# An LSTM step's attention sums, gate transpose and filler products rearranged in a four-layer kernel

## The chip, the cores and the metric

The kernel runs on one core of a Trainium2 chip, as one program. The metric is the device time of one execution in microseconds; lower is better. A core has TensorE (PE, matrix products, with weight loads shown apart as PEld), VectorE (DVE), ScalarE (ACT), GpSimd (POOL) and queues of DMA transfers, most of them issued by SyncE (SP). Each engine works through its own instructions in order and waits on semaphores for the others.

## What is computed

The reference is a chain of four layers on x (4 sequences of 512 tokens, 256 wide) with a context of 64 tokens per sequence. Each layer adds a gated attention-like part and a gated feed-forward part. Only the first layer matters here. Its attention part is a two-layer LSTM with attention over the context, and its feed-forward part is a mixture of 8 experts, of which the two best are summed per token:

```
for t in 512 steps:                                   # h, c: 4 x 256
    e     = tanh(ctx @ Wf + (h @ Wh)[:, None] + b)    # 4 x 64 x 256
    alpha = softmax(e @ v)                            # 4 x 64
    gates = [x_t, alpha @ ctx] @ W_ih0.T + h @ W_hh0.T + b
    i, f, g, o = split(gates)
    c = sigmoid(f) * c + sigmoid(i) * tanh(g)
    h = sigmoid(o) * tanh(c)
    (the second LSTM cell uses h and c of this step, not of an earlier one)
x = x + tanh(g_xattn[0]) * h2
x = x + tanh(g_ffn[0]) * mixture(layernorm(x))        # 8 experts, 256 -> 1024 -> 256, gelu
```

Everything is in fp32 in this part.

## The kernel before

The steps of the LSTM depend on each other, so `recurrence` calls `lstm_step` 512 times. The second cell and the mixture of experts of a block of 64 steps need nothing of later steps. They are cut into small tasks (`block_tasks`), which a planner, `Later`, puts into the holes of the following steps. `lstm_step` calls `later.fill(engine, budget)` at fixed places: each call hands out tasks of that engine, in the order of their kinds, until the budget is spent. For TensorE a mixture product (L720 up, L751 down: a 128x128 weight times 256 columns) costs 1; the three places are called slots A, B and C with budgets of 1, 2 and 2. An fp32 product is recorded as two passes. What is left behind the last step is put out by `later.drain()`, with nothing else beside it; then the next layers begin. All instructions of a step are pinned in program order, so each engine's queue has the order of the code.

One step, with the lines of the profile:

- L816 multiplies h by Wh (`psa`); VectorE transposes the result to `hw` (L821), which holds one number per partition, unit chunk c, and sequence.
- L825 adds h times W_hh to the gates in PSUM (`psf`). Then slot A.
- L833: two sums of VectorE, one for each pair p of sequences, add hw to the projected context `fproj`; the tile `e` is 128 partitions x [pair p, chunk c, sequence b in the pair, 64 context tokens]. L834 is the tanh of pair 0 (256 columns), L836 two tanh for pair 1, one per chunk (128 columns).
- L843: small products of `e` with v give the scores `psr` of each pair, pair 0 first, both chunks into one sum. Then slot B.
- L854 takes the maximum of a pair's scores, L855 the exp with its sum (the maximum enters as a bias operand). ScalarE may do one task of the planner here, among them the mixture's gelu (L730).
- L861 to L863 transpose and normalise to `alb`; L867 adds the attended context's share to `psf`. VectorE's task and slot C follow.
- L875 transposes `psf` to `gt`, all four gates at once. L474 starts the next step's gates with x's share. L878 is one tanh over the four gates (a sigmoid is a tanh of half its argument), L882 and L886 the new cell state, L888 its tanh `tcn`, L893 the new hidden state `hb`.
- If a task has changed ScalarE's table of functions (gelu), L891 runs a dummy exp on one element (`spare`) after `tcn`, so that the table of exp and tanh is loaded there and not in the path of the next step.

GpSimd copies the cell state (L894); SP's tasks, four a step, load the experts' weights and store blocks.

Of the kernel before, what the change touches and what calls it, by code (L numbers as in the profile page):

```python
# [24 lines left out]
AF = mybir.ActivationFunctionType  # L25
# [5 lines left out]
NB, S, D = 4, 512, 256  # L31
SC = 64
# [5 lines left out]
KD = D // P  # L38
NE = 8

SLOT_A, SLOT_B, SLOT_C = 1, 2, 2
ROUND = 1.5 * 2.0**23
F_MOE = (1024, 512, 1024)

# [96 lines left out]
def bc(ap, axis, n):  # L141

    ap = ap.unsqueeze(axis)
    shape = list(ap.shape)
    shape[axis] = n
    return ap.to_broadcast(shape)
# [214 lines left out]
def recurrence(net, w, pools):  # L361
# [22 lines left out]
    for t in range(S):  # L384
        i, u = divmod(t, P)
        if u == 0 and i + 1 < TPB:
            norm_x(net, later, w, pools, xb, i + 1)
        v = t % TB
        if v == 0:
            n = t // TB  # L390

            assert n < 3 or all(x["at"] for x in used[n - 3])
            hb = two.tile([P, 2, TB, NB], FP, name="hb", bufs=3)
            cb = two.tile([P, 2, TB, NB], FP, name="cb", bufs=3)
        if t % 32 == 0 and t and t // 32 + 1 < NJ:
            gates_of_block(net, later, w, pools, xb, ge, t // 32 + 1)
        lstm_step(net, pools["step"], ps, w, later, ge, t, h, hb[:, :, v], cb[:, :, v], ga[t % 2], ga[1 - t % 2])
        h = hb[:, :, v]
        if t > TB and t % 8 == 4:
            net.fill()  # L400
        if v == TB - 1:
            used.append(block_tasks(net, later, w, moe0, pools, n, hb, cb))
# [67 lines left out]
def gates_of_x(net, out, ge, t):  # L470

    sel = net.ident.rearrange("p (b t) -> p b t", b=NB)[:, :, t % 32]
    for q in range(4):
        net.tc.keep_in_program_order(net.nc.tensor.matmul(  # L474
            out[32 * q : 32 * q + NB, :], lhsT=sel, rhs=ge[t // 32][:, ts(q, 256)],
            start=True, stop=False,
        ))
# [330 lines left out]
def lstm_step(net, sp, ps, w, later, ge, t, h, hnew, cnew, ga, ganext):  # L808
    nc = net.nc
    pin = net.tc.keep_in_program_order  # L810
    psf = ps["f"]
    later.step += 1

    for c in range(2):
        for q in range(4):
            pin(nc.tensor.matmul(  # L816
                ps["a"][32 * q : 32 * q + NB, :], lhsT=h[:, c, :], rhs=w["wh"][:, c, ts(q, 64)],
                start=c == 0, stop=c == 1,
            ))
    hw = sp.tile([P, 2, 32], FP, name="hw")  # L820
    pin(nc.vector.transpose(hw.rearrange("p c b -> p (c b)"), ps["a"]))  # L821

    for c in range(2):
        for q in range(4):
            pin(nc.tensor.matmul(  # L825
                psf[32 * q : 32 * q + NB, :], lhsT=h[:, c, :], rhs=w["whh"][:, c, ts(q, 256)],
                start=False, stop=False,
            ))
    later.fill("PE", SLOT_A)

    e = sp.tile([P, 2, 2, 2, SC], FP, name="e")
    for p in range(2):
        pin(nc.vector.tensor_add(e[:, p], w["fproj"][:, p], bc(hw[:, :, ts(p, 2)], 3, SC)))  # L833
    pin(nc.scalar.activation(e[:, 0], e[:, 0], AF.Tanh))  # L834
    for c in range(2):
        pin(nc.scalar.activation(e[:, 1, c], e[:, 1, c], AF.Tanh))  # L836

    for p in range(2):
        for c in range(2):
            for b in range(2):  # L840
                ev = e[:, p, c, b].rearrange("p (i s) -> p i s", i=2)
                for i in range(2):
                    pin(nc.tensor.matmul(  # L843
                        ps["r"][p][ts(2 * b + i, 32), :], lhsT=w["vrep"][:, c, :],
                        rhs=ev[:, ::-1, :] if i else ev, start=c == 0, stop=c == 1,
                    ))
    later.fill("PE", SLOT_B)

    stat = sp.tile([P, 2, 3], FP, name="stat")
    al = sp.tile([P, 2, SC], FP, name="al")  # L850
    alT = sp.tile([P, 2, 32], FP, name="alT")
    alb = sp.tile([P, 2, NB], FP, name="alb")
    for p in range(2):
        pin(nc.vector.tensor_reduce(stat[:, p, 0:1], ps["r"][p], AX.X, ALU.max, negate=True))  # L854
        pin(nc.scalar.activation(  # L855
            al[:, p], ps["r"][p], AF.Exp, bias=stat[:, p, 0:1], accum_out=stat[:, p, 1:2]
        ))
    later.table = None
    later.fill("ACT", 1)
    for p in range(2):  # L860
        pin(nc.vector.transpose(alT[:, p], al[:, p, 0:32]))  # L861
        pin(nc.vector.reciprocal(stat[:, p, 2:3], stat[:, p, 1:2]))
        pin(nc.vector.scalar_tensor_tensor(  # L863
            alb[:, p], alT[:, p, 0:NB], stat[:, p, 2:3], w["own"][:, p], ALU.mult, ALU.mult
        ))
        for q in range(4):
            pin(nc.tensor.matmul(  # L867
                psf[32 * q : 32 * q + NB, :], lhsT=alb[:, p], rhs=w["fw"][:, p, ts(q, 256)],
                start=False, stop=p == 1,
            ))  # L870
    later.fill("DVE", 1)
    later.fill("PE", SLOT_C)

    gt = sp.tile([P, 8, 32], FP, name="gt")
    pin(nc.vector.transpose(gt.rearrange("p g b -> p (g b)"), psf))  # L875
    if t + 1 < S:
        gates_of_x(net, psf, ge, t + 1)
    pin(nc.scalar.activation(  # L878
        ga[:, 0:4].rearrange("p g c b -> p (g c) b"), gt[:, :, 0:NB], AF.Tanh, scale=0.5
    ))  # L880
    u = sp.tile([P, 2, 2, NB], FP, name="u")
    pin(nc.vector.scalar_tensor_tensor(  # L882
        u.rearrange("p g c b -> p g (c b)"), ga[:, 0:2].rearrange("p g c b -> p g (c b)"), 1.0,
        ga.rearrange("p (s x) c b -> p s x (c b)", x=2)[:, 1:3, 0], ALU.add, ALU.mult,
    ))
    pin(nc.vector.scalar_tensor_tensor(ganext[:, 4], u[:, 1], 0.5, u[:, 0], ALU.mult, ALU.add))  # L886
    tcn = sp.tile([P, 2, NB], FP, name="tcn")
    pin(nc.scalar.activation(tcn, ganext[:, 4], AF.Tanh, scale=0.5))  # L888
    if later.table:

        pin(nc.scalar.activation(w["spare"][0:1, 0:1], w["spare"][0:1, 1:2], AF.Exp))  # L891
        later.table = None
    pin(nc.vector.scalar_tensor_tensor(hnew, ga[:, 3], 1.0, tcn, ALU.add, ALU.mult))  # L893
    pin(nc.gpsimd.tensor_copy(cnew, ganext[:, 4]))  # L894
    later.fill("POOL", 1)
    later.fill("SP", 4)
# [1286 lines left out]
```

## Time and profile before

| what | value |
|---|---|
| median of 14 runs | 5411.22 us (5404.61 to 5414.55) |
| the profiled execution | 5411.6 us, its span 5409.9 us |
| busy share of the span | PE 85%, PEld 46%, DVE 45%, ACT 47%, POOL 9% |
| mean granted TensorE clock | 0.964 of full |
| first and last hidden state of the LSTM written at | 55.8 us and 3461.0 us |
| last product of the mixture behind the last step ends at | 3622 us |
| step length, plain median | 6.5 to 6.6 us |

The page gives, for the slowest core, the busy time of each engine, the same in 40 slices, the chain of work that ended last, and the costliest groups of instructions by line. A group's line has the number of instructions, their busy time, the mean ns of one, then the engine's idle time just before them and what ended most of it. The trace behind the page can be asked for the instructions in a stretch of time (the timeline) and for busy time by stretch (the windows). "Busy" for PE means that a product is in flight, not that the array is at its peak. A matrix product on four column groups at a time is noted 128*4 or 128*32.

### The profile page before, as it was taken

How to read it: one execution, taken by the hardware profiler on the slowest of the kernel's cores; microseconds unless marked ns; L12 is line 12 of the kernel's file. 1: busy time of each engine (PE TensorE's matmuls, PEld its weight loads, DVE VectorE, ACT ScalarE, POOL GpSimd, SP SyncE). 2: the span in 40 equal slices, each digit the busy share in tenths (PEclk: the TensorE clock that was granted, in tenths of full speed). 3: DMA queues.
4: the chain of work that ended last, by engine and by line, in shares of the span. 5: the costliest groups of instructions: out<-in, count | busy, mean ns of one | idle time of the engine just before them, and what ended most of it. 6: DMA issues, size and time to landing. Idle time of an engine off the chain costs nothing. (4 is left out here: it accounts for less than half of the span.)

```text
span 5409.9 us, 139195 instructions
## 1 busy us (share of the span) xinstructions
PE 4587.2 (85%) x57504; PEld 2502.5 (46%) x57504; DVE 2441.7 (45%) x9780; ACT 2532.8 (47%) x7118; POOL 465.9 (9%) x884
## 2 busy tenths in 40 slices
PE   5556699789999899999999989996989599979967
PEld 2222244334444344444444434673543366768744
DVE  3555555555555555555555555314433333221145
ACT  2233366555566556656556556511247366223212
POOL 1000100100000100000000000101011201130030
PEclk8999999999999999999999999997999799989978
DMA  5000012121122122122122111222454334553210
GB/s 194 2 2 2 2 72 94 64 75 72 73 97 111 42 88 95 72 82 80 65 89 95 72 63 44 89 89 74 168 175 149 132 118 142 201 175 137 95 53 8
DMA packets 117964, 480.46 MB, mean 89 GB/s; under 512 B 23473, under 2 KB 62787, under 8 KB 87939
## 3 DMA queue, kind: packets, MB, share of 16 engines
q1 hardware_dynamic: 105026, 437.85, 22.6%
q0 software_dynamic: 12288, 33.57, 1.8%
q8 instruction: 455, 7.45, 0.6%
q14 instruction: 195, 1.59, 0.1%
HBM read 434.65 MB, written 137.89 MB: 106 GB/s over the span
## 5 line engine op out<-in xcount | busy, mean ns | idle before, releaser
L867 PE MATMUL psf<-fw,alb 128*4 128x256 f32 x8192 | 537.7, 379 | 172.6 <-DVE alb L863 142.0
L720 PE MATMUL ps_up<-xm,ring 128*128 128x256 f32 x2048 | 614.8, 412 | 3.4 <-ACT h L730 3.3
L751 PE MATMUL ps_down<-ring,h 128*128 128x256 f32 x2048 | 582.2, 400 | 0.0
L825 PE MATMUL psf<-whh,hb 128*4 128x256 f32 x8176 | 537.4, 380 | 0.0
L720 PEld LDWEIGHTS ps_up<-xm,ring 128*128 128x128 f32 x2048 | 335.9, 188 | 226.7 <-issue 174.2
L855 ACT ACTIVATE al<-psr,stat 128x64 f32<-128x64 f32 x1024 | 313.3, 310 | 270.0 <-DVE stat L854 269.4
L834 ACT ACTIVATE e<-e 128x256 f32<-128x256 f32 x512 | 213.4, 417 | 465.2 <-DVE e L833 464.2
L751 PEld LDWEIGHTS ps_down<-ring,h 128*128 128x128 f32 x2048 | 357.8, 190 | 156.9 <-issue 111.5
L854 DVE TENSOR_REDUCE stat<-psr 128x1 f32<-128x64 f32 x1024 | 229.4, 225 | 416.8 <-PE psr L843 406.2
L833 DVE TENSOR_TENSOR e<-fproj,hw 128x256 f32<-128x256 f32 x1024 | 395.4, 427 | 17.6
L816 PE MATMUL psa<-wh,hb 128*4 128x64 f32 x8176 | 208.4, 219 | 230.0 <-DVE hb L893 229.4
L843 PE MATMUL psr<-e,vrep 128*32 128x64 f32 x16384 | 349.1, 224 | 49.1 <-ACT e L834 43.6
L894 POOL COPY cb<-ga 128x8 f32<-128x8 f32 x512 | 97.0, 189 | 3230.6 <-DVE ga L886 3230.6
L474 PE MATMUL psf<-ge,ident 128*4 128x256 f32 x4096 | 317.9, 382 | 65.4 <-DVE gt L875 65.2
L843 PEld LDWEIGHTS psr<-e,vrep 128*32 128x32 f32 x16384 | 261.4, 109 | 238.2 <-ACT e L834 230.4
L878 ACT ACTIVATE ga<-gt 128x32 f32<-128x32 f32 x512 | 116.8, 228 | 540.6 <-DVE gt L875 540.4
L875 DVE STREAM_TRANSPOSE gt<-psf 128x256 f32<-128x256 f32 x512 | 230.4, 450 | 302.0 <-PE psf L867 301.6
L1717 ACT ACTIVATE h<-featT,txtT 128x512 f32<-128x512 f32 x512 | 323.6, 710 | 72.9 <-PE psr L936 60.0
L867 PEld LDWEIGHTS psf<-fw,alb 128*4 128x4 f32 x8192 | 116.8, 84 | 518.2 <-DVE alb L863 516.8
L936 PE MATMUL ps_up<-xT,ring 128*128 128x256 f32 x1280 | 310.7, 395 | 42.4 <-DVE xT L1354 30.3
L816 PEld LDWEIGHTS psa<-wh,hb 128*4 128x4 f32 x8176 | 113.7, 85 | 487.3 <-DVE hb L893 487.3
L936 PEld LDWEIGHTS ps_up<-xT,ring 128*128 128x128 f32 x1280 | 246.2, 197 | 119.8 <-DVE xT L1354 31.9
(418 smaller groups left out, 6552.6 us busy)
## 6 DMA issues: line engine op xcount, KB each, us to landing
ring<-in_L_w_dram SPq DMA_DIRECT2D x208, 1024.0 KB, 4.8
ring<-in_L_w_dram SPq DMA_DIRECT2D x120, 512.0 KB, 4.0
res<-y SPq DMA_DIRECT2D x120, 128.0 KB, 1.7
rows_in<-rows SPq DMA_DIRECT2D x40, 256.0 KB, 3.8
rows_in<-rows SPq DMA_DIRECT2D x40, 128.0 KB, 2.9
rows<-in_x_dram SPq DMA_DIRECT2D x2, 1920.0 KB, 31.7
res<-in_x_dram SPq DMA_DIRECT2D x2, 1920.0 KB, 15.5
xtok<-in_x_dram SPq DMA_DIRECT2D x4, 512.0 KB, 6.0
```

The source lines that it names most:

```text
L474: net.tc.keep_in_program_order(net.nc.tensor.matmul(out[32 * q : 32 * q + NB, :], lhsT=sel, rhs=ge[t // 32][:, ts(q, 256)], start=True, st ...
L720: yield nc.tensor.matmul(cell["ps"][:, f % 2, :], lhsT=ex["w"][:, k, ts(f, P)], rhs=box["x"][:, k, :], start=k == 0, stop=k == KD - 1,)
L751: yield nc.tensor.matmul(cell["ps"], lhsT=ex["h"][:, f, ts(p, P)], rhs=ex["down"][:, f, :], start=f == 0, stop=f == 7,)
L816: pin(nc.tensor.matmul(ps["a"][32 * q : 32 * q + NB, :], lhsT=h[:, c, :], rhs=w["wh"][:, c, ts(q, 64)], start=c == 0, stop=c == 1,))
L825: pin(nc.tensor.matmul(psf[32 * q : 32 * q + NB, :], lhsT=h[:, c, :], rhs=w["whh"][:, c, ts(q, 256)], start=False, stop=False,))
L833: pin(nc.vector.tensor_add(e[:, p], w["fproj"][:, p], bc(hw[:, :, ts(p, 2)], 3, SC)))
L843: pin(nc.tensor.matmul(ps["r"][p][ts(2 * b + i, 32), :], lhsT=w["vrep"][:, c, :], rhs=ev[:, ::-1, :] if i else ev, start=c == 0, stop=c == ...
L855: pin(nc.scalar.activation(al[:, p], ps["r"][p], AF.Exp, bias=stat[:, p, 0:1], accum_out=stat[:, p, 1:2]))
L867: pin(nc.tensor.matmul(psf[32 * q : 32 * q + NB, :], lhsT=alb[:, p], rhs=w["fw"][:, p, ts(q, 256)], start=False, stop=p == 1,))
L875: pin(nc.vector.transpose(gt.rearrange("p g b -> p (g b)"), psf))
L936: return lambda *a, **k: self.tc.keep_in_program_order(fn(*a, **k))
L1717: nc.scalar.activation(h, featT[:, ec, :], AF.Tanh, bias=w["txtT"][:, ec, col : col + 1])
```

## The change

Four things change in `lstm_step`. First, a quarter of the attention's sums (pair 0, chunk 0) is not added by VectorE: two tanh of 64 columns, one per sequence, read `fproj` and take the column of hw as their bias operand. Second, the other three quarters are three sums of 128 columns, each followed by its own tanh, instead of two sums of 256 and tanh of 256, 128 and 128. Third, the transpose of the gates and their tanh are split into i, f, g (192 columns) and o (64 columns), and both tanh are queued before the next step's L474. Fourth, slot A is gone, so a step takes up to four mixture products instead of five; the number of products stays. In the changed kernel the bias tanh are L832, the three sums L836 and their tanh L837; further down line numbers shift by 1 to 4: the scores are L844, the maximum L855, exp L856, `alb` L864, L867 becomes L868, the transposes are L877, the gates' tanh L880, `u` L886, `tcn` L892, the dummy L895, the hidden state L897.

```diff
-SLOT_A, SLOT_B, SLOT_C = 1, 2, 2
+SLOT_B, SLOT_C = 2, 2
...
-    later.fill("PE", SLOT_A)
 
     e = sp.tile([P, 2, 2, 2, SC], FP, name="e")
-    for p in range(2):
-        pin(nc.vector.tensor_add(e[:, p], w["fproj"][:, p], bc(hw[:, :, ts(p, 2)], 3, SC)))
-    pin(nc.scalar.activation(e[:, 0], e[:, 0], AF.Tanh))
-    for c in range(2):
-        pin(nc.scalar.activation(e[:, 1, c], e[:, 1, c], AF.Tanh))
+    for b in range(2):
+        pin(nc.scalar.activation(
+            e[:, 0, 0, b], w["fproj"][:, 0, 0, b], AF.Tanh, bias=hw[:, 0, b : b + 1]
+        ))
+    for p, c in ((0, 1), (1, 0), (1, 1)):
+        pin(nc.vector.tensor_add(e[:, p, c], w["fproj"][:, p, c], bc(hw[:, c, ts(p, 2)], 2, SC)))
+        pin(nc.scalar.activation(e[:, p, c], e[:, p, c], AF.Tanh))
...
-    pin(nc.vector.transpose(gt.rearrange("p g b -> p (g b)"), psf))
+    for lo, hi in ((0, 6), (6, 8)):
+        pin(nc.vector.transpose(
+            gt[:, lo:hi].rearrange("p g b -> p (g b)"), psf[:, 32 * lo : 32 * hi]
+        ))
+        pin(nc.scalar.activation(
+            ga.rearrange("p g c b -> p (g c) b")[:, lo:hi], gt[:, lo:hi, 0:NB], AF.Tanh, scale=0.5
+        ))
     if t + 1 < S:
         gates_of_x(net, psf, ge, t + 1)
-    pin(nc.scalar.activation(
-        ga[:, 0:4].rearrange("p g c b -> p (g c) b"), gt[:, :, 0:NB], AF.Tanh, scale=0.5
-    ))
```

## The prediction

> **What bounds the kernel now.** I read the page's busy shares first (PE 85%, everything else below half), then its chain of waits. That chain covers only the last 200 us, in the layers behind the LSTM, which the change does not touch, so it says nothing here. The waits by engine then led to the LSTM lines: each step's engines wait for one another in turn. The timeline of one ordinary step, from one hidden state to the next, shows it (start us, duration us, engine, line, operation, tile; xN merges N instructions; in brackets the idle time before and who ended it):
>
> ```profile
> 1627.44 0.25 DVE L821 STREAM_TRANSPOSE hw<-psa 128x64 f32<-128x64 f32 x1 [0.53 <-PE psa L816]
> 1627.72 0.76 DVE L833 TENSOR_TENSOR e<-fproj,hw 128x256 f32<-128x256 f32 x2
> 1628.16 0.70 PE L720 MATMUL ps_up<-xm,ring 128*128 128x256 f32 x2
> 1628.24 0.42 ACT L834 ACTIVATE e<-e 128x256 f32<-128x256 f32 x1 [1.53 <-DVE e L833]
> 1628.57 0.49 ACT L836 ACTIVATE e<-e 128x128 f32<-128x128 f32 x2
> 1628.79 0.49 PEld L843 LDWEIGHTS psr<-e,vrep 128*32 128x32 f32 x32 [0.33 <-ACT e L834]
> 1629.29 0.45 DVE L854 TENSOR_REDUCE stat<-psr 128x1 f32<-128x64 f32 x2 [0.81 <-PE psr L843]
> 1630.76 0.22 DVE L863 SCALAR_TENSOR_TENSOR alb<-alT,stat,own 128x4 f32<-128x4 f32 x1
> 1631.73 0.45 DVE L875 STREAM_TRANSPOSE gt<-psf 128x256 f32<-128x256 f32 x1 [0.74 <-PE psf L867]
> 1632.28 0.23 ACT L878 ACTIVATE ga<-gt 128x32 f32<-128x32 f32 x1 [1.96 <-DVE gt L875]
> 1633.33 0.17 DVE L893 SCALAR_TENSOR_TENSOR hb<-ga,tcn 128x8 f32<-128x8 f32 x1 [0.34 <-ACT tcn L888]
> ```
>
> The reader is to see a serial chain in which the mixture's products (L720, L751) fill PE's holes. It is a chain of latencies: steps without any product take 6.50 us, steps with five 6.59. The one in slot A (at 1628.16) holds up the scores: L843 starts 0.13 after L834 ended, against 0.05 in steps without it.
>
> After the last step the products left over run with nothing beside them (windows; columns are length, then busy time and count of PE, PEld, DVE, ACT, POOL, then the granted clock):
>
> ```profile
> 3461.00:3541.00 80.00, 78.06 (x364) 66.42 (x363) 11.58 (x45) 28.13 (x59) 11.21 (x10) 1.00 0.39 135
> 3541.00:3622.00 81.00, 78.44 (x360) 67.72 (x358) 7.71 (x18) 17.83 (x42) 0.00 (x0) 1.00 0.23 80
> ```
>
> PE is busy for 156.5 of 161 us: here a product is paid in full.
>
> **Kinds of step.** Where a step has a gelu (L730), ScalarE loads its table before it and loads the old one back (L891) after `tcn`, into the next step:
>
> ```profile
> 2051.04 1.28 ACT L891 ACT_TABLE_LOAD   x1
> 2051.05 0.17 DVE L893 SCALAR_TENSOR_TENSOR hb<-ga,tcn 128x8 f32<-128x8 f32 x1 [0.28 <-ACT tcn L888]
> 2051.75 0.25 DVE L821 STREAM_TRANSPOSE hw<-psa 128x64 f32<-128x64 f32 x1 [0.53 <-PE psa L816]
> 2052.33 0.20 ACT L891 ACTIVATE spare<-spare 1x1 f32<-1x1 f32 x1
> ```
>
> After a gelu step ScalarE is free only 1.11 us after the hidden state, although hw is there at 0.78. Before, that was hidden, since the first tanh waited for VectorE's sum until 1.27. Four kinds by this, with their median length in the trace: plain 219 (105 at 6.50 without products, 114 at 6.59), gelu after plain 77 (6.66), gelu after gelu 139 (6.54), plain after gelu 77 (41 at 6.40, 36 at 6.26). Sum 3343 us; the trace has 60 us more in starts of blocks and table changes, which I leave as they are. In the changed program's order of instructions the counts are 259, 76, 101 and 76.
>
> **Part 1, the attention's sums.** Removed: two sums of 256 columns and three tanh. Added: two tanh of 64 columns with hw as bias, which need no sum, three sums and three tanh of 128. The price is that of a tanh with a bias operand from SBUF. The step has none, but a later layer has (groups by line, the second number behind the bar is the mean ns; then a timeline of four in a row):
>
> ```profile
> L1717 ACT ACTIVATE h<-featT,txtT 128x512 f32<-128x512 f32 x512 | 323.6, 710 | 72.9 <-PE psr L936 60.0 <-DVE featT L1705 12.8
> L836 ACT ACTIVATE e<-e 128x128 f32<-128x128 f32 x1024 | 254.6, 295 | 1.9 <-DVE e L833 1.9
> L855 ACT ACTIVATE al<-psr,stat 128x64 f32<-128x64 f32 x1024 | 313.3, 310 | 270.0 <-DVE stat L854 269.4
> ```
> ```profile
> 4008.68 2.56 ACT L1717 ACTIVATE h<-featT,txtT 128x512 f32<-128x512 f32 x4 [2.02 <-DVE featT L1705]
> ```
>
> Plain tanh: from `tcn` (8 columns, 209 ns) to L834 (256 columns, 417 ns) it is 0.84 ns a column; L836's two starts lie 0.20 apart. With a bias: median 707 ns for 512 columns, starts 0.61 apart (four in 2.56 with the last one's 0.71), so 0.10 of each is overlapped. 448 columns fewer at 0.84 leave 0.33, and the next start after 0.24. If the bias operand cost nothing it would be L836's 0.20 less 64 columns: 0.15. L855, also with a bias and 64 columns, but out of PSUM, takes 0.31, so 0.21. Not overlapped at all it would be 0.33. I take 0.24, as L1717 is the same operation out of the same memory; 0.15 and 0.33 are the ends.
>
> The Trainium skill ("ScalarE: Activation LUTs", What ACT_TABLE_LOAD costs) speaks against the change at this point: each pointer operand adds about 93 ns, and an activation with a pointer bias takes 280 ns and 0.833 a column, 333 ns here. By that estimate rather than L855's row the sum below is 25 us higher; it leaves my figure where it is.
>
> *Plain step*, in us after the hidden state. hw is complete at 0.78; ScalarE answers VectorE after 0.03, and after 0.06 more where it waits for two semaphores, as L834 did and the first bias tanh does. So the tanh start at 0.87, 1.11, 1.35 (ends 1.65), 1.55 and 1.75 (ends 2.05). VectorE's sums are never last: one of 256 takes 0.43, starts 0.34 apart; at the 1.04 ns a column between the transposes of hw (64 columns, 250 ns) and `gt` (256, 450) one of 128 takes 0.29, 0.21 apart, done by 1.10, 1.31 and 1.52. From the end of the last tanh of a half to its maximum L854 there are 0.44 (2.15 to 2.59 in steps without products). So the first L854 starts at 2.09, against 2.38 with a product in slot A and 2.30 without; the second at 2.49, which still meets the second exp's slot with 0.1 to spare. From the first L854 to `gt` it is 2.44, a chain on ACT and DVE. Behind L843's added waits on PE stand the other scores, slot B's products and L867, which needs `alb` (1.33 after the first L854: 3.42) and those products: last score pass 2.20, then 0.15, 0.32, 0.22, 0.22 and 0.31, the spacings of the trace: 3.42 too. So they just don't bind. `gt` starts at 4.53 instead of 4.82 or 4.74.
> *After a gelu*: the first bias tanh starts at 1.22 (1.11 and 0.11 for the small activation), 0.35 later than in a plain step. First L854 at 2.43, against 2.38 or 2.24; L867 by the same sum at 3.75 instead of 3.65, and from it 2.76 to the next hidden state, less part 2: 6.43.
> *Gelu steps*: here `ga` waits for table load and two gelus, which follow the second exp; they shift with it: from 3.40 to 3.14 after plain, from 3.34 to 3.48 after gelu.
>
> **Part 2, the gates.** `gt` takes 450 ns for 256 columns and hw 250 for 64, so 192 take 0.38: the tanh of i, f, g starts 0.07 earlier, wherever ScalarE is free, not in gelu steps. The second transpose and the tanh of o end about 0.9 after `gt` started; `tcn` wants ScalarE at 1.3: hidden, while nothing delays `tcn`. L474 waits for the second transpose, but PE is on slot C's products until later anyhow.
>
> **Part 3, four products.** Slot A's delay is in the lengths above. But the work stays: by the programs' orders 340 products lay behind the last step, and now 643 do. 303 products are 606 passes; successive passes in the drain start 0.216 apart: 131 us, and 160 us of drain have about 5 us of waits for ScalarE's gelus, so 136. Nothing can hide it: PE works in order and the next layer is behind it. The Trainium skill ("TensorE: Matmul & The Clock Gate", Back-to-back issue gap) would have N/2.4 + 2.5 = 109 ns for 256 columns, 66 us for the lot and a change that gains; the row, in fp32, is twice that and decides.
>
> **Sum.** New lengths: plain 6.59 - 0.29 - 0.07, rounded to 6.22 (6.50 - 0.21 - 0.07 is 6.22); gelu after plain 6.66 - 0.26 = 6.40; gelu after gelu 6.54 + 0.14 = 6.68; plain after gelu 6.43. 259 x 6.22 + 76 x 6.40 + 101 x 6.68 + 76 x 6.43 = 3261, 82 to 83 us less than 3343. The profiled execution took 5411.6 (span 5409.9), 0.4 above the median: 5411.6 - 83 + 136 - 0.4 = **5464 us**.
>
> **Rivals.**
> *Faster: the bias operand costs nothing.* At 0.15 per bias tanh each step is 0.19 shorter, 96 us in all: 5368. For it: the operand could be fetched while the engine waits. Against: L1717's starts are 0.61 apart in a full queue. It decides from 0.19 per bias tanh downward: there the step's gain pays for the drain.
> *Gain and drain cancel*, within 0.2%, which is about what a measurement of this kernel tells from no change: 0.18 to 0.20 per bias tanh: 5400 to 5422. L855's 0.21 with a drain at the bare 131 is still 5434.
> *Dearer: a bias tanh doesn't overlap* (0.33): 0.19 more in each step, 5561; ScalarE free only when the small activation has ended (1.31) adds 0.09 to 177 steps: 5480.
> *The change doesn't get its parts early*, if L843 waited for all of e: the order shows a wait at each part, so I give it nothing of its own.
>
> **Chances.** Forecast (5422 to 5505) 0.72; dearer 0.08; cancel 0.08; faster 0.12. The range 5400 to 5505 leaves out 0.2 at its two ends. Faster by over 0.2%: 0.12; within: 0.08; slower: 0.80.
>
> **What would show it.** Bias tanh 0.33 long, the next 0.24 after it; plain steps near 6.2 us; steps after a gelu no shorter; L843's first wait ended by the bias tanh or the (0,1) part; the last hidden state at about 3378 us instead of 3461, and then a drain of about 296 us at full clock instead of 161. Wrong if the tanh are spaced 0.15, if the gelu-after-gelu steps shorten, or if the granted clock falls in the longer drain.

## The result and the profile after

The changed kernel takes 5471.5 us (median of 6 runs, 5464.9 to 5477.2), against 5411.5 before (median of 28): ratio 1.0111, 95% interval 1.0101 to 1.0121. It is slower by 60 us; the forecast was 5464, slower by 53. The profiled execution took 5467.2, 55.6 more than that of before, so the traces account for 55.6 of the 60, and the profile is among the shorter runs.

Where it went, from the two traces (us):

| stretch | before | after | difference | forecast |
|---|---|---|---|---|
| up to the first hidden state | 55.8 | 54.3 | -1.5 | 0 |
| 511 further steps | 3405.2 | 3319.6 | -85.6 | -83 |
| products behind the last step, to VectorE's last sum of them (L758) | 160.6 | 303.2 | +142.6 | +136 |
| the next layers to the end of the span | 1788.3 | 1788.4 | +0.1 | 0 |

An ordinary step after the change, in the timeline (some of its lines are left out; start us, duration us, then as in the step shown of before; the hidden state before it was complete at 1615.58):

```profile
1616.10 0.25 DVE L821 STREAM_TRANSPOSE hw<-psa 128x64 f32<-128x64 f32 x1 [0.53 <-PE psa L816]
1616.39 0.70 DVE L836 TENSOR_TENSOR e<-fproj,hw 128x128 f32<-128x128 f32 x3
1616.45 0.59 ACT L832 ACTIVATE e<-fproj,hw 128x64 f32<-128x64 f32 x2 [1.07 <-DVE hw L821]
1616.85 0.99 PEld L844 LDWEIGHTS psr<-e,vrep 128*32 128x32 f32 x32 [0.46 <-ACT e L832]
1616.94 0.69 ACT L837 ACTIVATE e<-e 128x128 f32<-128x128 f32 x3
1617.67 0.23 DVE L855 TENSOR_REDUCE stat<-psr 128x1 f32<-128x64 f32 x1 [0.59 <-PE psr L844]
1619.15 0.22 DVE L864 SCALAR_TENSOR_TENSOR alb<-alT,stat,own 128x4 f32<-128x4 f32 x1
1620.11 0.52 DVE L877 STREAM_TRANSPOSE gt<-psf 128x192 f32<-128x192 f32 x2 [0.35 <-PE psf L868]
1620.59 0.34 ACT L880 ACTIVATE ga<-gt 128x24 f32<-128x24 f32 x2 [1.86 <-DVE gt L877]
1621.63 0.17 DVE L897 SCALAR_TENSOR_TENSOR hb<-ga,tcn 128x8 f32<-128x8 f32 x1 [0.34 <-ACT tcn L892]
```

The reader is to see three things. ScalarE now works from 0.87 us after the hidden state (1616.45) instead of 1.33, released by hw itself. The two bias tanh together take 0.59 us although they hold only 64 columns each, and the next tanh can start only 0.49 after the first of them. The first maximum starts at 2.09 instead of 2.38, and the hidden state is complete 6.22 us after the last one instead of 6.59.

The same engine in a step that follows a gelu (timeline of ScalarE; the hidden state was complete at 1596.23):

```profile
1596.05 1.28 ACT L895 ACT_TABLE_LOAD   x1
1597.35 0.20 ACT L895 ACTIVATE spare<-spare 1x1 f32<-1x1 f32 x1
1597.45 0.57 ACT L832 ACTIVATE e<-fproj,hw 128x64 f32<-128x64 f32 x2
1597.93 0.69 ACT L837 ACTIVATE e<-e 128x128 f32<-128x128 f32 x3
```

Here L832 has no bracket: it didn't wait for hw, it waited for its own engine. VectorE's sum could have been done in that time for nothing, so the bias should buy no start and cost its price; the experiment with four plain quarters below shows it.

Behind the last step (windows; columns as in those of before):

```profile
3384.00:3530.00 146.00, 140.85 (x648) 120.39 (x648) 16.61 (x55) 39.77 (x90) 11.20 (x10) 1.00 0.39 134
3530.00:3677.00 147.00, 143.20 (x657) 123.72 (x655) 11.67 (x26) 34.06 (x82) 0.00 (x0) 1.00 0.34 117
```

PE is busy for 284 of 293 us at full clock, nearly twice the time of before. Median lengths by kind of step, with what was forecast:

| kind | before | after | forecast |
|---|---|---|---|
| plain, with products / without | 6.59 / 6.50 | 6.23 / 6.23 | 6.22 |
| gelu after plain | 6.66 | 6.41 | 6.40 |
| gelu after gelu | 6.54 | 6.69 | 6.68 |
| plain after gelu, with products / without | 6.40 / 6.45 | 6.44 / 6.38 | 6.43 |

("With products" means at least two of them. The 6.45 is the middle of only 16 steps, which lie between 6.26 and 6.59.)

### The profile page after: what moved, and what is told of

The parts are those of the page before. It is cut to its first block, busy times and chain, and to the rows that moved or that the text cites. A ratio compares the mean times of both kernels' runs of the same rounds, so it can differ in the third digit from the quotient of the medians.

```text
span 5465.5 us, 142169 instructions
## 1 busy us (share of the span) xinstructions
PE 4736.5 (87%) x57504; PEld 2657.6 (49%) x57504; DVE 2443.7 (45%) x10804; ACT 2683.6 (49%) x8540; POOL 467.1 (9%) x884
## 3 DMA queue, kind: packets, MB, share of 16 engines
q1 hardware_dynamic: 105026, 437.85, 22.5%
## 5 line engine op out<-in xcount | busy, mean ns | idle before, releaser
L844 PE MATMUL psr<-e,vrep 128*32 128x64 f32 x16384 | 592.5, 231 | 49.5 <-ACT e L832 46.8
L868 PE MATMUL psf<-fw,alb 128*4 128x256 f32 x8192 | 537.8, 379 | 100.5 <-DVE alb L864 95.9
L844 PEld LDWEIGHTS psr<-e,vrep 128*32 128x32 f32 x16384 | 390.2, 108 | 409.8 <-ACT e L832 286.8
L720 PE MATMUL ps_up<-xm,ring 128*128 128x256 f32 x2048 | 546.9, 398 | 8.7 <-ACT h L730 8.3
L751 PE MATMUL ps_down<-ring,h 128*128 128x256 f32 x2048 | 542.5, 396 | 0.0
L832 ACT ACTIVATE e<-fproj,hw 128x64 f32<-128x64 f32 x1024 | 297.9, 337 | 362.8 <-DVE hw L821 362.7
L880 ACT ACTIVATE ga<-gt 128x24 f32<-128x24 f32 (+1 forms) x1024 | 170.7, 214 | 569.5 <-DVE gt L877 568.3
L855 DVE TENSOR_REDUCE stat<-psr 128x1 f32<-128x64 f32 x1024 | 230.2, 225 | 446.8 <-PE psr L844 446.8
L720 PEld LDWEIGHTS ps_up<-xm,ring 128*128 128x128 f32 x2048 | 356.7, 189 | 143.2 <-issue 79.8
L856 ACT ACTIVATE al<-psr,stat 128x64 f32<-128x64 f32 x1024 | 321.5, 314 | 180.7 <-DVE stat L855 180.7
L877 DVE STREAM_TRANSPOSE gt<-psf 128x192 f32<-128x192 f32 (+1 forms) x1024 | 263.3, 295 | 319.1 <-PE psf L868 318.6
L816 PE MATMUL psa<-wh,hb 128*4 128x64 f32 x8176 | 208.8, 220 | 205.1 <-DVE hb L897 201.6
L836 DVE TENSOR_TENSOR e<-fproj,hw 128x128 f32<-128x128 f32 x1536 | 361.6, 291 | 17.6
L474 PE MATMUL psf<-ge,ident 128*4 128x256 f32 x4096 | 318.4, 382 | 57.3 <-DVE gt L877 57.3
L837 ACT ACTIVATE e<-e 128x128 f32<-128x128 f32 x1536 | 354.7, 293 | 2.6 <-DVE e L836 2.1
L816 PEld LDWEIGHTS psa<-wh,hb 128*4 128x4 f32 x8176 | 114.0, 86 | 462.9 <-DVE hb L897 462.9
L868 PEld LDWEIGHTS psf<-fw,alb 128*4 128x4 f32 x8192 | 122.8, 84 | 421.1 <-DVE alb L864 411.9
```

Of the source, the lines that this page charges most:

```text
L474: net.tc.keep_in_program_order(net.nc.tensor.matmul(out[32 * q : 32 * q + NB, :], lhsT=sel, rhs=ge[t // 32][:, ts(q, 256)], start=True, st ...
L720: yield nc.tensor.matmul(cell["ps"][:, f % 2, :], lhsT=ex["w"][:, k, ts(f, P)], rhs=box["x"][:, k, :], start=k == 0, stop=k == KD - 1,)
L751: yield nc.tensor.matmul(cell["ps"], lhsT=ex["h"][:, f, ts(p, P)], rhs=ex["down"][:, f, :], start=f == 0, stop=f == 7,)
L816: pin(nc.tensor.matmul(ps["a"][32 * q : 32 * q + NB, :], lhsT=h[:, c, :], rhs=w["wh"][:, c, ts(q, 64)], start=c == 0, stop=c == 1,))
L836: pin(nc.vector.tensor_add(e[:, p, c], w["fproj"][:, p, c], bc(hw[:, c, ts(p, 2)], 2, SC)))
L837: pin(nc.scalar.activation(e[:, p, c], e[:, p, c], AF.Tanh))
```

## The experiments

All ratios are to the kernel before on the same chip; each kernel's steps and drain are read from its own trace.

**The gates' split alone.** In the kernel before, only this:

```diff
-    pin(nc.vector.transpose(gt..., psf))
+    for lo, hi in ((0, 6), (6, 8)):
+        pin(nc.vector.transpose(gt[:, lo:hi]..., psf[:, 32 * lo : 32 * hi]))
+        pin(nc.scalar.activation(ga...[:, lo:hi], gt[:, lo:hi, 0:NB], AF.Tanh, scale=0.5))
     if t + 1 < S:
         gates_of_x(net, psf, ge, t + 1)
-    pin(nc.scalar.activation(ga[:, 0:4]..., gt[:, :, 0:NB], AF.Tanh, scale=0.5))
```

> The kernel before with the split of the gates' transpose and tanh alone. Theory (the gain of the split is 0.07 us wherever ScalarE is free, nothing in steps with a gelu): 219 plain steps and 77 after a gelu gain 0.07 each, 21 us, about 5390. Rival (the second transpose and tanh delay the new cell state or the next step's gates, or the split is hidden): no gain, 5411 or more.

Measured: 5387.3 us, ratio 0.9953 (0.9939 to 0.9966). Plain steps 6.59 to 6.51 and 6.50 to 6.43, plain after gelu 6.40 to 6.33, both gelu kinds unchanged within 0.01; the 511 steps are 23.4 us shorter. The split is a gain, of the size and in the kinds of step that the working named.

**Four products alone.** In the kernel before, slot A left out:

```diff
-    later.fill("PE", SLOT_A)
```

> The kernel before with slot A left out alone: four products a step, the sums and the gates as before. Theory (a product moved behind the last step is paid in full, 303 of them about 140 us; slot A's delay is 0.08 to 0.14 in the steps that have a product there): steps -38, drain +142, about 5516; the drain about 303 us long. Rival (the change's loss sits in the steps and the drain is partly hidden by the next layer): below 5450.

Measured: 5530.0 us, ratio 1.0214 (1.0198 to 1.0229). The drain is 304.4 us long, the steps 25.9 shorter (38 were expected: the medians fell by the 0.08 to 0.14 stated, to 6.50 in plain steps, 6.42 in gelu after gelu and 6.26 in plain after gelu, but the steps that lie off the medians add up to 12 us more than before, 5 of them in the second step of all, which takes 27.5 instead of 22.5). The window over the drain:

```profile
3433.50:3737.90 304.40, 292.89 (x1335) 250.37 (x1333) 29.91 (x85) 78.19 (x180) 11.23 (x10) 0.99 0.36 124
```

So this part alone loses 2.1%, nearly twice the whole change, and the other parts win back about half. The rival that the loss sits in the steps is out.

**Slot A back.** In the changed kernel:

```diff
-SLOT_B, SLOT_C = 2, 2
+SLOT_A, SLOT_B, SLOT_C = 1, 2, 2
...
+    later.fill("PE", SLOT_A)
+
     e = sp.tile([P, 2, 2, 2, SC], FP, name="e")
```

> The changed kernel with slot A put back where it was: five products. Theory (a product in slot A holds the scores up until 1.88 us after the hidden state, so the early parts are of no use where it stands; plain steps with a product 6.52, without 6.23; steps after a gelu as in the changed kernel, 6.43 and 6.68; gelu after plain 6.66): steps 11 us below those of the kernel before, drain as before, about 5401. Rival (the parts' gain and the products are independent): steps as in the changed kernel and the drain as before, about 5330.

Measured: 5394.6 us, ratio 0.9964 (0.9952 to 0.9976): below the kernel before, but far from 5330. The steps are 20.3 us shorter than before, where 11 were expected. A plain step with a product is 6.51, one without 6.23. The timeline of such a step (hidden state complete at 1598.96; lines are 2 higher than in the changed kernel):

```profile
1599.83 0.59 ACT L834 ACTIVATE e<-fproj,hw 128x64 f32<-128x64 f32 x2 [1.07 <-DVE hw L821]
1600.21 0.70 PE L720 MATMUL ps_up<-xm,ring 128*128 128x256 f32 x2
1600.32 0.69 ACT L839 ACTIVATE e<-e 128x128 f32<-128x128 f32 x3
1600.84 0.49 PEld L846 LDWEIGHTS psr<-e,vrep 128*32 128x32 f32 x32 [0.33 <-ACT e L839]
1601.34 0.45 DVE L857 TENSOR_REDUCE stat<-psr 128x1 f32<-128x64 f32 x2 [0.88 <-PE psr L846]
```

The first bias tanh is ready at about 1.22, but PE's queue holds the product first, and the scores start at 1.88 as before the change; the maximum starts at 2.38. The bracket names ScalarE, which had long delivered the first part: the product is what stood in the way. Early parts and a product ahead of the scores exclude each other. With slot A in place the rearranged sums bring nothing over the split of the gates alone: 5394.6 against 5387.3, and steps of 3384.9 us in all against 3381.8.

**Four plain quarters.** In the changed kernel the bias goes:

```diff
-    for b in range(2):
-        pin(nc.scalar.activation(
-            e[:, 0, 0, b], w["fproj"][:, 0, 0, b], AF.Tanh, bias=hw[:, 0, b : b + 1]
-        ))
-    for p, c in ((0, 1), (1, 0), (1, 1)):
+    for p, c in ((0, 0), (0, 1), (1, 0), (1, 1)):
```

> The changed kernel with the two bias tanh replaced by a fourth sum of VectorE and a plain tanh of 128 columns. Theory (a bias tanh occupies ScalarE for 0.24, so two of them cost more than one of 128; after a gelu ScalarE is the late one): plain steps 0.03 longer, gelu after gelu 6.41 instead of 6.68, plain after gelu 6.17 instead of 6.43; 32 us less, about 5439. Rival (the bias saves VectorE's first sum on the path and costs nothing): 0.03 or more longer in every step, 5488.

Measured: 5445.5 us, ratio 1.0057 (1.0042 to 1.0072), 26 us below the changed kernel by the medians, where 32 were expected: the steps are 23.2 us shorter, the drain 3.3 longer. Plain steps 6.28 instead of 6.23, gelu after plain 6.46 instead of 6.41; but gelu after gelu 6.41 instead of 6.69 and plain after gelu 6.16 instead of 6.44. After a reload of the table (ScalarE's timeline; four tanh of 128 columns in 0.89 us, against 1.17 in the changed kernel from the first bias tanh to the last tanh):

```profile
1599.21 0.20 ACT L891 ACTIVATE spare<-spare 1x1 f32<-1x1 f32 x1
1599.32 0.89 ACT L833 ACTIVATE e<-e 128x128 f32<-128x128 f32 x4
```

Here, too, ScalarE starts 0.11 after the start of the small activation, so after a reload the bias buys no earlier start. The part of the change that moved work to ScalarE is a loss by itself, in the 177 steps where ScalarE is the late engine.

**The price of the operand.** The four quarters again, each tanh with a bias of zeros (the spare's second column), which changes no value:

```diff
-        pin(nc.scalar.activation(e[:, p, c], e[:, p, c], AF.Tanh))
+        pin(nc.scalar.activation(e[:, p, c], e[:, p, c], AF.Tanh, bias=w["spare"][:, 1:2]))
```

> The four plain quarters, each tanh with a bias operand of zeros from SBUF: the price of the operand alone. Theory (about 0.09 each, in duration and in spacing): tanh 0.386 long and 0.295 apart instead of 0.293 and 0.20; plain steps 0.26 longer than without, gelu steps 0.37; about 5595. Rival (the operand is fetched at no cost): as without it, 5439.

Measured: 5619.7 us in its one run; about 5595 was expected. The group of this tanh with and without the operand (mean ns is the second number behind the bar), first this kernel, then the four plain quarters:

```profile
L833 ACT ACTIVATE e<-e,spare 128x128 f32<-128x128 f32 x2048 | 652.0, 388 | 481.3 <-DVE e L832 481.1
```
```profile
L833 ACT ACTIVATE e<-e 128x128 f32<-128x128 f32 x2048 | 462.7, 296 | 480.8 <-DVE e L832 480.8
```

After a reload (ScalarE's timeline, to be set beside the 0.89 us of the four plain quarters):

```profile
1662.32 0.20 ACT L891 ACTIVATE spare<-spare 1x1 f32<-1x1 f32 x1
1662.42 1.26 ACT L833 ACTIVATE e<-e,spare 128x128 f32<-128x128 f32 x4
```

388 against 296, and the starts lie 0.292 us apart instead of 0.199: a bias operand costs 92 ns of duration and 93 of the engine's time. That is the figure of the Trainium skill ("ScalarE: Activation LUTs", What ACT_TABLE_LOAD costs), about 93 ns for each pointer operand, shown here by an edit of nothing else. Steps with a gelu and steps after one are 0.37 longer and plain steps without products 0.27, close to what was expected; plain steps with products are 0.36 longer instead of 0.26. In one of these PE has no idle time before L864 (the attended context's share) and is on slot B's products until then:

```profile
1684.06 1.13 PE L751 MATMUL ps_down<-ring,h 128*128 128x256 f32 x4
1684.66 0.22 DVE L860 SCALAR_TENSOR_TENSOR alb<-alT,stat,own 128x4 f32<-128x4 f32 x1
1685.12 1.05 PE L864 MATMUL psf<-fw,alb 128*4 128x256 f32 x16
```

`alb` is there at 1684.88, so the later scores have pushed slot B's products past it.

**Three products in slot C.** The changed kernel with its fifth product behind the attended context instead of ahead of the scores:

```diff
-SLOT_B, SLOT_C = 2, 2
+SLOT_B, SLOT_C = 2, 3
```

> The changed kernel with three products in slot C instead of two, so five a step but none ahead of the scores. Theory (products cost nothing where PE waits for the gates; the loss is the drain's alone): drain back to about 162 us; plain steps with products 0.07 longer (PE reaches the next step's first product at 6.35 instead of 6.28), plain after gelu 0.12 to 0.19 longer, gelu steps unchanged; about 5368. Rival (the steps have no room for a fifth product anywhere): each step with a product 0.43 longer, 5460 or more.

Measured: 5360.2 us, ratio 0.9899 (0.9883 to 0.9916), 111 us below the changed kernel by one number. The drain is 164.6 us. Plain steps with products are of two sorts: the 42 that follow an ordinary plain step have a median of 6.28, 0.05 longer where 0.07 was expected; the 49 that follow a plain step after a gelu have 6.39, 0.16 longer. Plain after gelu itself, expected 0.12 to 0.19 longer, stays at 6.43, so the delay that was expected there comes out one step later. Gelu after plain is 6.46, 0.05 longer, and gelu after gelu 6.69, as in the changed kernel.

**The kernel before with slot A's product moved to slot C.**

```diff
-SLOT_A, SLOT_B, SLOT_C = 1, 2, 2
+SLOT_B, SLOT_C = 2, 3
...
-    later.fill("PE", SLOT_A)
```

> The kernel before with slot A's product moved to slot C, nothing else. Theory: scores no longer held up, steps 6.50 plain, 6.58 gelu after plain, 6.40 gelu after gelu, 6.26 to 6.38 plain after gelu, drain as before: about 5380. Rival (slot A's product is hidden as it stands): 5411 or more.

Measured: 5388.0 us, ratio 0.9950 (0.9933 to 0.9966); the drain is 164.7 us, the steps are 25.6 us shorter. In the 42 plain steps with products that follow an ordinary plain step the product is hidden behind the attended context: 6.50, as without any, where it cost 0.09 ahead of the scores. The 49 that follow a plain step after a gelu stay at 6.59; there L816 starts 0.15 after the hidden state instead of 0.05. Both kinds after a gelu gain 0.12 to 0.14 and gelu after plain 0.09. So slot A's product had not been hidden in any of these kinds.

**Quarters and three products in slot C**, two of the edits together, in the changed kernel:

```diff
-SLOT_B, SLOT_C = 2, 2
+SLOT_B, SLOT_C = 2, 3
...
-    for b in range(2):
-        pin(nc.scalar.activation(
-            e[:, 0, 0, b], w["fproj"][:, 0, 0, b], AF.Tanh, bias=hw[:, 0, b : b + 1]
-        ))
-    for p, c in ((0, 1), (1, 0), (1, 1)):
+    for p, c in ((0, 0), (0, 1), (1, 0), (1, 1)):
```

> The changed kernel with four plain quarters instead of the bias, and three products in slot C. Theory: plain 6.26 and 6.33, gelu after plain 6.45, gelu after gelu 6.41, plain after gelu 6.35, drain about 162 us: 5325, below both kernels. Rival (bias is worth having): above the changed kernel with three products in slot C.

Measured: 5322.3 us, ratio 0.9830 (0.9814 to 0.9847), below both kernels. The time came within 3 us of the expected 5325, in part by luck: gelu after plain is 6.51 instead of 6.45, and the delay expected in plain after gelu (6.35) isn't there (6.16); it shows in the plain step behind it, which is 6.44. What holds that step up at its start is PE (timeline of PE; the hidden state was complete at 1581.20):

```profile
1579.50 1.56 PE L751 MATMUL ps_down<-ring,h 128*128 128x256 f32 x6
1580.99 0.62 PE L474 MATMUL psf<-ge,ident 128*4 128x256 f32 x8
1581.42 0.41 PE L816 MATMUL psa<-wh,hb 128*4 128x64 f32 x16
```

L816 has no bracket and starts 0.22 after the hidden state, where it used to start 0.05 after it: it stands behind L474, and that behind three products. That is the 0.16 by which 6.44 exceeds 6.28. The step before it is a plain step after a gelu, in which L864 starts only 2.68 before the hidden state, against 2.80 in an ordinary plain step, so PE is later with slot C's products; 49 steps with products stand behind such a one, with a median of 6.44. In the 42 that follow an ordinary plain step L816 starts 0.10 after the hidden state, and their median is 6.32, as expected (6.33).

**Bias only where ScalarE is free.** On top of that, the form is chosen per step when the program is built; `late` says that the step before has reloaded the table:

```diff
+        self.late = False
...
+    head = [] if later.late else [0, 1]
+    for b in head:
+        pin(nc.scalar.activation(
+            e[:, 0, 0, b], w["fproj"][:, 0, 0, b], AF.Tanh, bias=hw[:, 0, b : b + 1]
+        ))
-    for p, c in ((0, 0), (0, 1), (1, 0), (1, 1)):
+    for p, c in ((0, 0), (0, 1), (1, 0), (1, 1))[len(head) // 2 :]:
...
+    later.late = bool(later.table)
     if later.table:
```

> Three products in slot C, and the two bias tanh only in steps in which ScalarE is free when hw is ready; steps that follow a reload of ScalarE's table take the four plain quarters. Theory (the bias form wins 0.05 where ScalarE waits for hw, and loses 0.28 where hw waits for ScalarE): 0.05 below the kernel with quarters everywhere (5322) in some 296 steps, 14 us, about 5308. Rival (one form is better everywhere): 5322 or more.

Measured: 5303.4 us, ratio 0.9796 (0.9783 to 0.9809), the fastest here: 2.0% below the kernel before and 3% below the changed one. The steps are 15.3 us shorter than with quarters everywhere, the drain the same: plain steps and gelu after plain are 0.05 shorter each, both kinds after a gelu unchanged. So each form wins in its own kind of step.

**Four products in slot C**, with quarters everywhere:

```diff
-SLOT_B, SLOT_C = 2, 3
+SLOT_B, SLOT_C = 2, 4
```

> The kernel with four plain quarters and four products in slot C instead of three. Theory (PE has no hole left in slot C: the step with three is already held up by it by 0.16 in plain steps): the drain falls by 39 products, 17 us, while each step that takes a sixth product gets some 0.3 to 0.43 longer, so slower than 5322, 5340 to 5400. Rival (there is still room): about 5305.

Measured: 5400.8 us, ratio 0.9975 (0.9965 to 0.9984), just above the expected 5340 to 5400. The drain falls only to 155.3 us, by 9 instead of 17: it holds 39 products fewer, but PE's pauses of more than 0.45 in it grew by 5 us. Plain steps with products grow from 6.44 to 6.87 where they follow a plain step after a gelu and from 6.32 to 6.75 elsewhere, gelu after plain from 6.51 to 6.95 and gelu after gelu from 6.41 to 6.70. 0.43 is a whole product: in plain steps slot C has room for two products and most of a third, and no more.

## Why the prediction was right, and where it was off

- **The bias tanh** (0.33 long, the next after 0.24): 0.332 long, 0.238 apart after a gelu and 0.254 in plain steps, where the first is 0.348 long. The row L1717 of another layer, cut to 64 columns, carried the whole of part 1. The edit with the zero bias shows the cause as well as the size.
- **The kinds of step.** All four lengths came within 0.01 us. The decision that mattered was to keep apart where ScalarE waits for hw and where hw waits for ScalarE: the plain step's gain of 0.37 taken for all 512 would have been 189 us, more than the drain's cost, and the wrong sign.
- **The first rival** (the bias costs nothing, 5368) fell: 0.24 is above the 0.19 at which the step's gain would have paid for the drain. "Gain and drain cancel", from 0.18 to 0.20 per bias tanh, fell with it. The two rivals for a dearer bias fell as well: the tanh overlap, and the first one starts 0.11 after the start of the dummy, not at its end. So did the last, that the parts don't come early: in the step shown, L844 starts 0.40 after the first bias tanh did, before the sum for the last part has ended.
- **The gates**: 0.07 in 23 us of steps, none with a gelu, as worked out.
- **The drain** is the term that was mis-sized: 142.6 us instead of 136. The passes were right (606 of 0.216 are 131). The rest was not 5 us, as much again as before, but 11.6. Starts of passes more than 0.45 apart exceed the even spacing by 13.0 us in all after the change and by 4.2 before; starts 0.30 to 0.45 apart, at switches between kinds of product, are 32 instead of 16. What PE waited for in the drain, first after the change, then before (us in total, times, longest):

```profile
PE ps_up L720 <- ACT h L730: 8.3, 10, 1.2
PE ps_ct L683 <- ACT h L730: 2.1, 1, 2.1
```
```profile
PE ps_up L720 <- ACT h L730: 3.3, 4, 1.2
```

These are 7.1 us more: the first gelus behind the last step stand behind two table loads, and PE waits 2.1 us for them; the other waits for gelus went from four to ten. The spacing of 109 ns for 256 columns that the prediction worked out from the Trainium skill ("TensorE: Matmul & The Clock Gate", Back-to-back issue gap), applied to each recorded pass, would have made the drain's growth 66 us. That section gives the formula for the isolated gap of a matmul and has no figure for fp32; the recorded passes here are 216 ns apart, and the growth was 142.6 and 143.8 us in the changed kernel and in the one with slot A left out alone.
- **The steps** gained 85.6 instead of 83, and the start 1.5; these and the drain's error of 6.6 the other way partly cancel and leave the profiled execution 2.6 above its forecast. The median lies 4.3 above the profiled execution, where the prediction had it 0.4 below, as before the change.

## What to carry to other kernels

When a chain of small steps hides work of another stage, count what a step gives back: a product that leaves its hole is paid in full where it lands, and here the shorter step (85 us) did not pay for 303 of them (143 us); ask first whether there is another hole behind another wait, and look one step further for its price: what the third product in slot C costs shows only in the step behind it. A fused operand is not free because it removes an instruction: it moves time to the engine that reads it, so look in which steps that engine is the late one, and let the program take the other form there.

## What the runs showed of the hardware that was not expected

- Between the last pass of a product on column groups (128*4) and the first on the full array lie 0.31 us, the second pass follows after 0.32 instead of 0.216, and the way back takes 0.31 again. With one product in slot A the passes on either side of it start 0.945 and 1.883 us after the hidden state: 0.94 us for what costs 0.43 in a row of its like.
- Two transposes in place of one cost VectorE 0.52 us instead of 0.45, and the second was hidden in every kernel that had it: there `tcn` waited for VectorE in all 512 steps.
- The six runs of the changed kernel spread over 12 us, and the longer ones show a lower granted clock (0.961 at 5475.5 of span, 0.964 at 5463.1). What sets it was not tried.
